# Dividing the queries, folding the sums into the projection, and a column of ones for the softmax denominators

## The chip, the cores and the metric

The kernel runs on one core of a Trainium2 chip. The metric is the device time of one execution in microseconds (us). Before the change the median of three runs is 7744.9 us (7739.69 to 7749.79). The engines are called as in the profile: PE is the matrix engine (PEld its weight loads), DVE the vector engine, ACT the scalar engine, POOL the GpSimd engine, SP the engine that issues most DMAs.

## What is computed

Four images of 256 channels and 64 x 64 pixels (4096 positions) go through four blocks, each added to its input after a group norm: a block with deformable sampling and a feed-forward, linear attention on several scales, a 3 x 3 convolution with binarised weights, and a non-local block with pooled keys. The change touches the second and the fourth:

```python
# layer 1: linear attention, heads of 8 channels
ms = jnp.concatenate([qkv, agg], axis=1)          # qkv, and a 5x5 depthwise aggregate of it
t = ms.reshape(B, -1, 3 * DIM, H * W)
q, k, v = jnp.split(t, 3, axis=2)
q = jax.nn.relu(q)
k = jax.nn.relu(k)
vk = jnp.einsum('bhdn,bhen->bhde', v, k)
out = jnp.einsum('bhde,bhen->bhdn', vk, q)
denom = jnp.einsum('bhe,bhen->bhn', k.sum(-1), q)
out = out / (denom[:, :, None, :] + EPS)
out = out.reshape(B, -1, H, W)
out = conv2d(out, proj_w, 'SAME')                 # 1x1
out = jax.nn.relu(out * proj_bn_scale[:, None, None] + proj_bn_bias[:, None, None])
...
# layer 3: pooled attention, 4096 queries, 1024 keys after a 2x2 max pool
m1 = jnp.einsum('bnc,bcm->bnm', theta1, phi1)
m1 = jax.nn.softmax(m1, axis=2)
m2 = jnp.einsum('bnm,bmc->bnc', m1, gi1)
m4 = _conv1x1(m2.reshape(B, c, H, W), wz_w, wz_b)
return m4 + ox
```

## The kernel before

All numbers are f32. Channels lie on the 128 partitions (256 channels are two groups), positions along the free dimension in blocks of 512 (eight per image).

**The works.** Python generators write the instructions: `sample` (deformable sampling), `feedforward`, `layer1` (linear attention), `layer2` (the convolution), `layer3` (pooled attention). `beside` (L1182) runs a leading generator and advances others beside it in proportion to costs that they yield. In the ordered stages the order on PE, DVE, ACT and POOL is the order of writing; nothing is reordered on an engine later. The end of the program (the last convolution with the end of the third image's work, and the last pooled attention) is left to a scheduler.

**The stages.** Sampling of image 0 stands beside the first convolutions of images 1 to 3; of image 1 beside feed-forward and linear attention of image 0; of images 2 and 3 beside feed-forward and linear attention of the image before and convolution plus pooled attention of the image before that. After sampling come the feed-forward and linear attention of image 3, from the latter's start beside the convolution and pooled attention of image 2, then the convolution and the pooled attention of image 3.

**Sampling** is 288 rounds per image, each of four indirect DMAs that POOL issues (L591) into one of seven buffers g. PE multiplies each g into acc (L598); ACT copies acc to at every second round (L603), which frees a half of acc; PE transposes at (L608). When all seven buffers are in use, POOL waits for the matmuls of L598.

**Linear attention.** `rows` (L790) makes q, k and v per block (matmuls L805) into padded tiles pad; `depthwise` (L169) runs the 5 x 5 aggregate, 25 steps per chunk of 1024 positions on DVE (L178). Other work is put into a list `later`, one entry of which is written out between the DVE steps. `outer` (L842) transposes keys and values (L850, L851) and adds their products over positions into `sums` (L857). `summed` (L869) runs once when the sums of a tile index t are complete, for kind 0 (qkv) and kind 1 (aggregate): it masks the sums to the head blocks (`ln`, L873) and lays the key sums out as weights `ld`. `output` (L879) runs per chunk of 1024 queries: `dens` makes the denominators (matmul L889, on DVE an add and a reciprocal into rd); then for each half h, four `head` entries and two `proj` entries. A head multiplies ln with the queries (num, L898), spreads the reciprocals over the channels of a head (rden, L901), copies num to ot on ACT (L903) and multiplies ot with rden on DVE (L904). `proj` multiplies four ot with the projection weights pw (L910), and ACT (pr, L912) and DVE (L913) finish. There are 32 heads per image, 128 in all.

**Pooled attention.** `first` and `then` make th (queries), ph (keys) and gt (values). Then for each tile of 128 queries (32 per image): scores s against 1024 keys (L1135), their maxima on DVE (L1136, L1137), the exponential on ACT with its sums accumulated (L1142), eight transposes on PE (L1150), two copies on ACT (L1151), eight matmuls with gt (L1155), and on DVE the sum of two partial denominators (L1144), the reciprocal (L1145) and the scaling of the result into m2 (L1156). After four tiles, L1161 multiplies m2 with the output weights.

**PSUM.** The mm pool has three banks, taken in turn by `ps()`: num, rden, s, pt, ps, po and the others share them, and a matmul waits until whoever read the bank three takings before has finished.

## Time and profile before

| | us |
|---|---|
| median of three runs | 7744.9 |
| profiled execution, its own time | 7735.88 |
| its span, first to last instruction | 7734.1 |
| PE busy (share of the span) | 5939.0 (77%) |
| DVE busy | 5191.6 (67%) |
| POOL busy | 5026.2 (65%) |
| ACT busy | 2200.4 (28%) |
| gathers L591: first to last start | 133.2 to 6250.0 |
| num matmuls L898, all forms, records summed | 161 |
| ACT copies L903 | 75.0 |
| DVE multiplies L904 | 87.4 |
| PE waits for the copies at L603 (acc <- ACT) | 711.0 |
| ACT waits for num | 333.4 |

Busy times are those of records. An f32 matmul leaves two records that overlap, so PE's busy time is larger than its work. A share of the whole span is a mean over stages that are bound by different engines; the stages have to be read one by one. "A waits for B" is idle time of A that ended when B's instruction finished.

### The profile page before, as it was taken

The numbers are of one execution on the slowest core, as the hardware profiler recorded it, in microseconds if no ns is written. First come the engines' busy times: TensorE is split into PE (matmuls) and PEld (weight loads), VectorE is DVE, ScalarE is ACT, GpSimd is POOL, SyncE is SP. The second block draws the span as 40 slices with busy tenths as digits, with TensorE's granted clock in tenths as the row PEclk, the third lists the DMA queues.
The fourth block names the chain that finished last, engine by engine and source line by source line (L and its number), as shares of the span: only waits on it lengthen the run. The fifth ranks groups of instructions, "written<-read, shape, count | busy, mean of one in ns | idle before, by whom it ended". The sixth has DMA issues, their size and how long they took to land. (4 is left out here: it accounts for less than half of the span.)

```text
span 7734.1 us, 94959 instructions
## 1 busy us (share of the span) xinstructions
PE 5939.0 (77%) x36000; PEld 3468.1 (45%) x36000; DVE 5191.6 (67%) x6665; ACT 2200.4 (28%) x4879; POOL 5026.2 (65%) x4870
## 2 busy tenths in 40 slices
PE   5666666579766677898777778987777889967899
PEld 2333333334333333446544434465444435744487
DVE  6555553644787887238888892289888933999634
ACT  1111111212222222223233222222333323655415
POOL 2777777777777777777777667777776621966220
PEclk7676776779777778999898899998888999978999
DMA  6564664565544444555544455465444432210121
GB/s 188 152 178 137 172 173 139 160 183 157 162 122 125 125 141 132 165 151 163 149 144 133 122 154 165 136 170 157 142 134 128 123 123 65 75 52 33 63 87 58
DMA packets 744344, 1031.45 MB, mean 133 GB/s; under 512 B 354128, under 2 KB 459984, under 8 KB 742352
## 3 DMA queue, kind: packets, MB, share of 16 engines
q0 software_dynamic: 221184, 604.27, 27.2%
q1 hardware_dynamic: 522704, 421.10, 18.2%
q8 instruction: 285, 4.67, 0.3%
q14 instruction: 171, 1.40, 0.1%
HBM read 856.39 MB, written 168.61 MB: 133 GB/s over the span
## 5 line engine op out<-in xcount | busy, mean ns | idle before, releaser
L591 POOL DMA_INDIRECT g<-tab,sl x4608 | 4492.3, 975 | 1757.4 <-issue 1273.2
L178 DVE SCALAR_TENSOR_TENSOR agg<-pad,vec,agg 128x1024 f32<-128x1024 f32 x2280 | 2934.0, 1287 | 60.6
L598 PE MATMUL acc<-g,wm 128*32 128x128 f32 x18432 | 1266.6, 319 | 1241.6 <-ACT at L603 711.0
L598 PEld LDWEIGHTS acc<-g,wm 128*32 128x32 f32 x18432 | 623.2, 121 | 1927.9 <-ACT at L603 951.2
L1036 PE MATMUL ps<-xd,w 128*128 128x256 f32 x3072 | 712.3, 385 | 7.3 <-DVE x L1016 2.8
L582 DVE TENSOR_TENSOR wm<-con,sl 128x768 f32<-128x768 f32 x384 | 365.8, 953 | 420.3 <-PE acc L598 400.7
L1036 PEld LDWEIGHTS ps<-xd,w 128*128 128x128 f32 x3072 | 577.6, 193 | 107.3 <-issue 29.8
L618 ACT COPY dT<-dp 64x128 f32<-64x128 f32 x1152 | 296.7, 258 | 1044.3 <-PE dp L608 705.6
L730 PE MATMUL ps<-x2f,f 128*128 128x512 f32 x1024 | 479.0, 615 | 4.0 <-ACT f L705 4.0
L740 PE MATMUL ps<-hm,f 128*128 128x512 f32 x1024 | 462.0, 600 | 0.0
L715 DVE SCALAR_TENSOR_TENSOR hm<-ps,vec,lk 128x512 f32<-128x512 f32 x256 | 192.2, 751 | 400.4 <-ACT lk L732 397.3
L805 PE MATMUL ps<-xr,qw 128*128 128x512 f32 x768 | 450.7, 718 | 11.5 <-DVE ot L904 4.1
L987 POOL TENSOR_TENSOR xd<-xp 128x640 f32<-128x640 f32 x64 | 79.5, 1269 | 477.3 <-ACT xp L999 382.9
L603 ACT COPY at<-acc 128x256 f32<-128x256 f32 x576 | 214.4, 372 | 490.0 <-PE acc L598 477.9
L732 ACT ACTIVATE lk<-ps,low 128x512 f32<-128x512 f32 x256 | 175.9, 687 | 594.9 <-PE ps L730 593.6
L631 PE MATMUL po<-dT,ow 128*128 128x288 f32 x1024 | 312.2, 455 | 13.4 <-ACT dT L626 6.5
L608 PE MATMUL dp<-ident,at 128*128 128x128 f32 x1152 | 267.6, 320 | 66.8 <-ACT dT L618 54.7
L194 POOL TENSOR_TENSOR ak<-ak,m 128x1024 f32<-128x1024 f32 x96 | 228.1, 2376 | 131.0 <-ACT m L193 126.7
L1155 PEld LDWEIGHTS ps<-gt,pT 128*128 128x128 f32 x2048 | 278.5, 215 | 60.7 <-issue 34.3
L1155 PE MATMUL ps<-gt,pT 128*128 128x128 f32 x2048 | 291.0, 302 | 7.1 <-ACT pT L1151 7.0
L730 PEld LDWEIGHTS ps<-x2f,f 128*128 128x128 f32 x1024 | 191.3, 194 | 230.1 <-issue 216.9
L194 POOL TENSOR_TENSOR av<-av,m 128x1024 f32<-128x1024 f32 x96 | 226.9, 2363 | 101.1 <-ACT m L193 96.7
(246 smaller groups left out, 7723.0 us busy)
## 6 DMA issues: line engine op xcount, KB each, us to landing
g<-tab,sl POOLq DMA_INDIRECT x4608
x<-x SPq DMA_DIRECT2D x128, 512.0 KB
xr<-x SPq DMA_DIRECT2D x96, 512.0 KB
tab<-xo SPq DMA_DIRECT2D x192, 128.0 KB
x<-in_x SPq DMA_DIRECT2D x32, 512.0 KB
y<-yc SPq DMA_DIRECT2D x32, 512.0 KB
yb<-y SPq DMA_DIRECT2D x64, 256.0 KB
x<-yb SPq DMA_DIRECT2D x64, 256.0 KB
```

Of the source, the lines that this page charges most:

```text
L178: nc.vector.scalar_tensor_tensor(to, s, wt, acc, ALU.mult, ALU.add)
L194: nc.gpsimd.tensor_tensor(acc, acc, m, ALU.add)
L582: nc.vector.tensor_tensor(wm, self.con("own").unsqueeze(1).unsqueeze(1).to_broadcast(sh), blocks[b][:, r:r + WR, G:].unsqueeze(3).to_broad ...
L591: nc.gpsimd.indirect_dma_start(out=g[:, i, :], out_offset=None, in_=table, in_offset=bass.IndirectOffsetOnAxis(ap=sl.bitcast(I32)[:, r, i: ...
L598: nc.tensor.matmul(acc[32 * i:32 * i + 32, :], wm[:, r4, 4 * i + 2 * x:4 * i + 2 * x + 2, :], g[:, i, x * P:(x + 1) * P], start=x == 0, st ...
L618: nc.scalar.copy(dT[b][hs, :, r:r + UR], dp[u][hs, :, :, s, :].rearrange("p v g o -> p g v o"))
L631: nc.tensor.matmul(po[m][:, 0:BR * OB], self.ow[:, k, m * P:(m + 1) * P], dT[b][:, k].rearrange("p r o -> p (r o)"), start=k == 0, stop=k ...
L730: nc.tensor.matmul(ps, f1[:, k, m * P:(m + 1) * P], x2[:, k], start=k == 0, stop=k == KT - 1)
L740: nc.tensor.matmul(ps, f2[:, k, m * P:(m + 1) * P], hm[:, k], start=k == 0, stop=k == 4 * KT - 1)
L805: nc.tensor.matmul(ps, qw[:, k, m * P:(m + 1) * P], x[:, k], start=k == 0, stop=k == KT - 1)
L1036: nc.tensor.matmul(ps[:, e], w[:, k, t, 2 * half + e, m * P:(m + 1) * P], v[:, 2 * half + e, k, t:t + 8], start=i % 6 == 0, stop=i % 6 == 5)
L1155: nc.tensor.matmul(ps[:, 0:P], pT[:, m], gt[:, m], start=m == 0, stop=m == 7)
```

## The change

In linear attention the order of the factors is swapped when the sums are formed, so that they come out as values by keys. `summed` multiplies each masked sum into the 128 rows of the projection weights that belong to it (comb), and copies the product over pw. A head then has no num matmul and no ACT copy: DVE multiplies the queries with the spread reciprocals, and the projection runs on these. `ld` and the denominators stay as they are.

In pooled attention gt gets a 129th column of ones. The result's matmul is 129 columns wide, and its last column is the denominator; the exponential doesn't accumulate any more, DVE has only a reciprocal of that column, and ACT scales the result into m2.

```diff
                 def added(i):
                     for j in range(2):
-                        nc.tensor.matmul(sums[:, t, kind], kts[i][:, 0, j], kts[i][:, 1, j],
+                        nc.tensor.matmul(sums[:, t, kind], kts[i][:, 1, j], kts[i][:, 0, j],
                                          start=first and i + j == 0, stop=last and i + 1 == len(at) and j == 1,
                                          skip_group_check=True)
...
             def summed(t):
 
+                pc = self.ps("comb").rearrange("p (e o) -> p e o", e=2)
                 for kind in range(2):
                     j = 2 * kind + t
                     nc.vector.tensor_tensor(ln[:, j], sums[:, t, kind], self.con("bd"), ALU.mult)
...
+                for kind in range(2):
+                    nc.tensor.matmul(pc[:, kind], ln[:, 2 * kind + t], pw[:, 2 * kind + t], start=True, stop=True)
+                    nc.vector.tensor_copy(pw[:, 2 * kind + t], pc[:, kind])
...
                 def head(h, j):
                     if not j:
                         xv.append(self.block(bp, self.x3_d[n], 2 * c + h, "xq", bufs=1))
-                    pn = self.ps("num")
-                    nc.tensor.matmul(pn, ln[:, j], qh[h][j], start=True, stop=True)
                     hs, i = slice(64 * (j // 2), 64 * (j // 2) + 64), 2 * h + j % 2
                     pb = self.ps("rden")
                     nc.tensor.matmul(pb, self.con("sel")[hs, i * P:(i + 1) * P], rd[0][hs], start=True, stop=True)
                     ot[h, j] = bp.tile([P, 512], F32, name="ot", tag="kt", bufs=4)
-                    nc.scalar.copy(ot[h, j], pn)
-                    nc.vector.tensor_tensor(ot[h, j], ot[h, j], pb, ALU.mult)
+                    nc.vector.tensor_tensor(rw(ot[h, j]), qh[h][j], rw(pb), ALU.mult)
...
-            gt = sp.tile([P, 8, P], F32, name="gt")
+            gt = sp.tile([P, 8, P + 1], F32, name="gt")
+            nc.vector.memset(gt[:, :, P:], 1.0)
...
-                nc.vector.tensor_tensor(gt[:, b], ps[:, P:2 * P], gb, ALU.add)
+                nc.vector.tensor_tensor(gt[:, b, 0:P], ps[:, P:2 * P], gb, ALU.add)
...
                     pe = bp.tile([P, M], F32, name="pe")
-                    den = bp.tile([P, 3], F32, name="den3")
                     for i in range(2):
-                        nc.scalar.activation(pe[:, i * 512:(i + 1) * 512], s[i], AF.Exp, bias=mx[:, 2:3], accum_out=den[:, i:i + 1])
+                        nc.scalar.activation(pe[:, i * 512:(i + 1) * 512], s[i], AF.Exp, bias=mx[:, 2:3])
                     yield 2
-                    nc.vector.tensor_tensor(den[:, 2:3], den[:, 0:1], den[:, 1:2], ALU.add)
-                    nc.vector.reciprocal(den[:, 2:3], den[:, 2:3])
...
                     ps = self.ps()
                     for m in range(8):
-                        nc.tensor.matmul(ps[:, 0:P], pT[:, m], gt[:, m], start=m == 0, stop=m == 7)
-                    nc.vector.tensor_scalar(m2[:, j * P:(j + 1) * P], ps[:, 0:P], den[:, 2:3], None, ALU.mult)
+                        nc.tensor.matmul(ps[:, 0:P + 1], pT[:, m], gt[:, m], start=m == 0, stop=m == 7)
+                    rden = bp.tile([P, 1], F32, name="rden")
+                    nc.vector.reciprocal(rden, ps[:, P:P + 1])
+                    nc.scalar.activation(m2[:, j * P:(j + 1) * P], ps[:, 0:P], AF.Copy, scale=rden)
```

The yields and their costs are unchanged, and so is the order of all other instructions in the ordered stages. In the unordered end the scheduler's order on PE and ACT moves a little around the tiles of pooled attention.

## The prediction

> **What bounds the kernel now.** I read the page's slices first, then who GpSimd (POOL) waits for in stretches, then busy time by stretch, then the groups that the change touches. First the slices (each digit tenths of 193 us):

> ```profile
> PE   5666666579766677898777778987777889967899
> DVE  6555553644787887238888892289888933999634
> POOL 2777777777777777777777667777776621966220
> PEclk7676776779777778999898899998888999978999
> ```

> POOL issues the gathers of sampling. One takes 0.946 us and the next starts about 0.30 us later, so 76 us busy in 100 is its full pace, and slices 2 to 32 are paced by it as long as it keeps that pace. The 6s and single low windows are where it didn't. Who held it (us, times, longest), in 2700-3160, 4200-4700 and 5800-6260 us:

> ```profile
> POOL g L591 <- issue: 102.0, 335, 0.3
> ...
> POOL g L591 <- PE acc L598: 0.3, 1, 0.3
> ...
> POOL g L591 <- issue: 88.0, 289, 0.3
> POOL g L591 <- PE acc L598: 69.3, 32, 7.6
> ...
> POOL g L591 <- issue: 82.5, 271, 0.3
> POOL g L591 <- PE acc L598: 67.3, 30, 6.5
> ```

> The reader is to see that the same attention output costs nothing in the second image's sampling (0.3 us of wait), and that in the third's and fourth's, where the pooled attention runs as well, POOL runs out of gather buffers for 69 and 67 us, because TensorE is late. Busy time of PE, PE loads, DVE, ACT, POOL by stretch:

> ```profile
> 3900.00:4000.00 100.00, 65.55 (x533) 44.14 (x531) 91.97 (x113) 32.77 (x82) 76.24 (x79) 0.89 0.46 132
> 4400.00:4500.00 100.00, 81.41 (x502) 43.59 (x501) 85.75 (x110) 33.12 (x78) 59.63 (x62) 0.91 0.44 127
> 6000.00:6100.00 100.00, 87.56 (x526) 46.48 (x525) 85.71 (x103) 31.95 (x75) 65.25 (x68) 0.92 0.41 117
> 6950.00:7000.00 50.00, 35.52 (x146) 23.36 (x147) 48.92 (x54) 32.20 (x50) 34.88 (x15) 0.90 0.13 43
> 7050.00:7100.00 50.00, 47.08 (x142) 23.82 (x143) 45.62 (x53) 23.93 (x36) 22.83 (x10) 0.94 0.13 42
> 7650.00:7700.00 50.00, 50.00 (x294) 39.90 (x293) 24.72 (x65) 28.53 (x66) 0.00 (x0) 1.00 0.19 64
> ```

> At 4400 and 6000 no engine is full: PE, DVE and ACT wait for each other in a fixed order. At 6950 (sampling over) DVE is full; at 7050, with attention output, PE and DVE share the bound; at 7650 PE is full. The groups:

> ```profile
> L898 PE MATMUL num<-pad,ln 128*128 128x512 f32 x128 | 79.5, 704 | 1.5 <-ACT pT L1151 1.1 <-DVE ot L904 0.4
> L903 ACT COPY ot<-num 128x512 f32<-128x512 f32 x128 | 75.0, 586 | 333.6 <-PE num L898 333.4
> L904 DVE TENSOR_TENSOR ot<-ot,rden 128x512 f32<-128x512 f32 x128 | 87.4, 683 | 94.8 <-PE rden L901 90.7 <-ACT yb L642 4.1
> L1142 ACT ACTIVATION_READ_ACCUMULATOR pe<-s,mx 128x1 f32 x256 | 50.4, 197 | 0.0
> L1156 DVE TENSOR_SCALAR m<-ps,den 128x128 f32<-128x128 f32 x128 | 44.6, 349 | 110.6 <-PE ps L1155 110.0
> ```

> ACT stands 333 us waiting for num: not work, but while it waits, the copies of acc behind it (L603) are late, and PE waited 711 us for those.

> [...] two 512-column f32 matmuls of L1161 (four records of about 0.6 us each) take 1.72 us from start to next start, so one costs 0.86 us at full clock, and I price with that, not with the records. [...] sixteen records of L1155 take 1.78 us, 0.111 each for 128 columns, so a 129th column is an estimated 0.9 ns per record. [...]

> **The change part by part.**

> *Heads (32 per image).* Gone: one 512-column matmul (0.86 us, about 0.95 at the clock of 0.9 there), one ACT copy (0.586) and one of two PSUM banks taken from a rotation of three. The DVE multiply stays; its source is now q (partly strided rows) and no longer waits for ACT. I keep 0.68, bounds 0.62 to 0.75.

> *Summed (2 per image).* New: two comb matmuls of 256 columns (630 records of L1036 in 135.99 us: 0.43 per matmul), two DVE copies from PSUM (L1019's 0.42), and DVE waits some 0.7 for the first. About 1.5 each, 3 us per image where DVE is full. If PE is behind, a wait like the 5 us seen elsewhere comes in: bound 10. PE in turn waits at comb for DVE, with the acc matmuls behind it; seven gather buffers cover that.

> *Pooled tiles (32 per image).* DVE loses an add (0.154), a reciprocal (0.163) and the scaling (0.350), and gains a reciprocal from PSUM, not shown before: 0.16 like L1145's, bounds 0.13 to 0.25. Net -0.50. ACT loses two accumulator reads (0.2 each, about 0.08 each of pitch, as the next exp overlaps them) and gains a 128-element scaled copy[...]. PE gains 16 x 0.9 = 14 ns; bounds 0 and, should an odd row length cost, double, 1.8 us. The new ACT copy waits for DVE's reciprocal; behind it on ACT stand the next exp and L603, for which PE waits. A memset is once per image.

> Now by stage, since a microsecond counts only where it isn't under POOL.

> First two samplings: POOL at full pace, or no touched code. 0.

> Third sampling. num has 43 records in 4300-4600, two per matmul, so 21 heads: 21 x 0.95 = 20 us of PE, 21 x 0.586 = 12 of ACT, and 12 tiles (96 transposes) x 0.50 = 6 of DVE. POOL is short of its pace by 12.3+16.7+11.6 busy us there, 53 us of time. These overlap in one ring, so I count the largest, 20. Before it, 3800-4300, POOL lacks 22 busy us, 29 of time, DVE the fullest; 20 tiles x 0.50 = 10, of which I take 8, one window being at full pace. Sum 28.

> Fourth sampling, the same reading: 24 heads in 5900-6200 give 23, I take 22; the tiles before 8. Sum 30.

> After sampling. DVE full in 6900-7250: 21 tiles x 0.50 = 10.5. In 7000-7345 DVE waits 18.8 us for rden and 31.3 for ACT's pr, which waits for PE; about 35 of the 50 lie before 7250, and PE has 22 of the 32 heads (19 us) less there: I take 15. In 7250-7350 PE has 46.9 and 42 of 50; 10 heads x 0.86 = 8.6. Less 3 for summed. Sum 31. What is late next: the depthwise chains on DVE, then PE.

> The last pooled attention, 196 us, is full on PE: +32 x 0.014 = 0.5, and 0.3 for reciprocal plus ACT copy in the tail. Its DVE and ACT savings are hidden by PE; without that cover they would be worth 16 us.

> Sum: -28 -30 -31 +1 = -88. The profiled execution took 7735.9 (span 7734.1), so 7648; the median of the runs, 7744.9, stands 9 above it, so **7657 us**. With each share taken low (heads 8 per stage, tiles 4, after sampling 12) it is -36; taken high (heads 35, tiles 15, after 45), -145: 7709 and 7600.

> **Rivals.**

> *DVE keeps the bound.* The 85 to 92 in 100 of DVE say that it sets most rounds and PE's saving falls in gaps. Then 12+11 tiles and the tiles before count half (14), after sampling 10.5+8.6, less 3 per image in stages that count (9), and half of the wait relief (8): about -32, 7713. Against: where DVE alone is busy (3900) POOL is at full pace; it falls only where heads come in.

> *The ring opens.* If the copy that stalled ACT was the hinge, most of the 53+29 us and the like of the fourth sampling come back, some 100, with 50 after: -150, 7595. For: the 711 us of PE waits on L603. Against: DVE at 86 leaves little.

> *The new ACT copy takes the place of the old.* In order on ACT, it waits until DVE reaches the reciprocal, often behind three taps of 1.29 us (3.9). If 96 tiles lose 1.3 us each to late L603 copies, that is +125-88 = +37, 7782. It decides from 0.92 us per tile. For: DVE is the lagging engine. Against: ACT already waits for DVE's maxima in 95 of 128 tiles (339 us), and the reciprocal stands before the next maxima in DVE's order; ACT is busy a third of the time.

> *The waits only change name.* Gathers stay as late for another reason: 7745.

> **How the numbers follow.** Forecast 0.50, DVE keeps the bound 0.20, ring opens 0.15, ACT copy 0.10, no effect 0.05. Within 0.2% (15 us) a measurement can't be told from no change. Faster is the sum of the first three, 0.85; same 0.05; slower 0.10. The range 7600 to 7735 leaves out the ACT copy and no effect (0.15) and the far part of the open ring (0.05).

> **What would show it.** Right: POOL's waits for acc fall from 69 and 67 to about 45 each; ACT has no 333 us before ot; DVE's busy falls by about 64 us less 7; the last gather starts some 55 us before 6250; the last 196 us stay within 2. Wrong: a long ACT wait for DVE's reciprocal with PE waiting on L603 more than 711; L1155 records over 0.12 us; DVE still at 98 in 100 with the same end; PEclk lower where PE got work taken away.

## The result, and the profile after

| | before | after |
|---|---|---|
| median, us (ten runs each) | 7746.37 | 7758.41 |
| lowest to highest, us | 7739.69 to 7757.17 | 7748.26 to 7775.53 |
| ratio after/before, 95% interval | | 1.0017 [1.0007, 1.0027] |
| profiled execution, us | 7735.88 | 7748.26 |
| last gather starts at, us | 6250.0 | 6283.4 |
| mean granted clock of PE | 0.851 | 0.839 |

A gain of 88 us was forecast; the change lost 12, less than 0.2%. Both profiled executions took some 10 us less than the median of their kernel. The work that was to go has gone. These are the page's busy times of after (busy us, share of the span, instructions) and, of its slices, the row of PE's granted clock (tenths, one digit per 194 us):

```profile
PE 5899.6 (76%) x35776; PEld 3468.2 (45%) x35776; DVE 5126.8 (66%) x6429; ACT 2148.7 (28%) x4623; POOL 5035.0 (65%) x4870
...
PEclk7676776779777677999888888999888889988999
```

DVE's busy time fell by 65 us (57 forecast) and ACT's by 52. PE has 224 matmul records fewer (256 for num gone, 32 for comb and the like come), but its busy time fell by only 39 us, though the num records alone summed to 161. The PEclk row (before's stands in the prediction) hints at the reason: of slices 17 to 34, eleven read 9 before and seven after. The windows below show it sharper.

Who waits for whom in after, over the span (total us, times, longest us):

```profile
PE acc L598 <- ACT at L603: 711.4, 370, 26.2
ACT m L1157 <- DVE rden L1156: 361.0, 108, 15.3
POOL g L591 <- PE acc L598: 297.7, 182, 11.2
```

ACT's 333 us before ot are gone. In their place stand 361 us before m: ACT waits for DVE's late reciprocal, up to 15.3 us at a time, with the copies of acc behind it. PE's wait for those copies has stayed where it was (711.0 before). POOL's wait for PE has risen (269.8 before), not fallen; in the two stretches where the forecast had 69 and 67 us and expected 45, it is 85 and 81.

Where the time went, stage by stage. The marks are the starts of gathers, counted from 0, so that the stretches hold the same sampling in every kernel: "pooled" is where pooled attention stands beside sampling, "crowded" where linear attention's heads stand there too. Each of the first two rows is one profiled execution, so differences below some 5 us mean little by themselves.

| us | third: pooled (2880-3136) | third: crowded (3136-3456) | fourth: pooled (4032-4300) | fourth: crowded (4300-4607) | last gather to last pooled attention | last stage |
|---|---|---|---|---|---|---|
| before | 331.3 | 467.4 | 344.4 | 448.3 | 1315.2 | 168.9 |
| after | 337.8 | 482.6 | 349.5 | 462.8 | 1287.1 | 175.9 |
| difference | +6.5 | +15.2 | +5.1 | +14.5 | -28.1 | +7.0 |

Before gather 2880 and between the two groups of stretches, after gains 8 us. So these four stretches, which were to give 58 us, took 41 more, and the last gather starts 33 us later; the stretch after them gave what was forecast; the last stage took 7 more. The two crowded stretches by windows, before (length, then busy time of PE, PE loads, DVE, ACT and POOL with counts, granted clock, DMA share, GB/s):

```profile
4221.70:4689.10 467.40, 364.42 (x2396) 197.33 (x2396) 382.82 (x452) 141.22 (x343) 309.47 (x320) 0.88 0.46 137
5801.70:6250.00 448.30, 346.03 (x2278) 184.72 (x2276) 369.03 (x437) 134.49 (x326) 296.61 (x307) 0.89 0.43 128
```

and after:

```profile
4221.80:4704.40 482.60, 356.11 (x2340) 198.22 (x2340) 377.78 (x421) 128.36 (x296) 313.19 (x321) 0.83 0.44 133
5820.60:6283.40 462.80, 341.49 (x2242) 188.42 (x2241) 366.05 (x409) 122.44 (x283) 299.97 (x307) 0.83 0.42 124
```

Less work on PE, DVE and ACT, a longer stretch, and a clock of 0.83 where it was 0.88 and 0.89.

### The profile page after: what moved, and what is told of

The parts are those of the page before. It is cut to its first block, busy times and chain, and to the rows that moved or that the text cites. A ratio compares the mean times of both kernels' runs of the same rounds, so it can differ in the third digit from the quotient of the medians.

```text
span 7746.5 us, 94023 instructions
## 1 busy us (share of the span) xinstructions
PE 5899.6 (76%) x35776; PEld 3468.2 (45%) x35776; DVE 5126.8 (66%) x6429; ACT 2148.7 (28%) x4623; POOL 5035.0 (65%) x4870
## 5 line engine op out<-in xcount | busy, mean ns | idle before, releaser
L591 POOL DMA_INDIRECT g<-tab,sl x4608 | 4502.1, 977 | 1781.0 <-issue 1267.5
L598 PE MATMUL acc<-g,wm 128*32 128x128 f32 x18432 | 1288.4, 322 | 1248.4 <-ACT at L603 711.4
L598 PEld LDWEIGHTS acc<-g,wm 128*32 128x32 f32 x18432 | 631.2, 122 | 1955.1 <-ACT at L603 941.0
L603 ACT COPY at<-acc 128x256 f32<-128x256 f32 x576 | 214.1, 372 | 488.6 <-PE acc L598 474.3
L732 ACT ACTIVATE lk<-ps,low 128x512 f32<-128x512 f32 x256 | 175.9, 687 | 595.5 <-PE ps L730 595.5
L1154 PE MATMUL ps<-gt,pT 128*128 128x129 f32 x2048 | 303.6, 310 | 7.3 <-ACT pT L1150 6.9
L1137 PE MATMUL s<-ph,th 128*128 128x512 f32 x512 | 274.2, 649 | 22.8 <-DVE r L1164 6.3
```

The lines of the kernel that those rows point to most:

```text
L591: nc.gpsimd.indirect_dma_start(out=g[:, i, :], out_offset=None, in_=table, in_offset=bass.IndirectOffsetOnAxis(ap=sl.bitcast(I32)[:, r, i: ...
L598: nc.tensor.matmul(acc[32 * i:32 * i + 32, :], wm[:, r4, 4 * i + 2 * x:4 * i + 2 * x + 2, :], g[:, i, x * P:(x + 1) * P], start=x == 0, st ...
L1137: nc.tensor.matmul(s[i], tv[:, 4 * b + j], ph[:, i * 512:(i + 1) * 512], start=True, stop=True)
L1154: nc.tensor.matmul(ps[:, 0:P + 1], pT[:, m], gt[:, m], start=m == 0, stop=m == 7)
```

## The experiments

Three things had to be told apart: what the linear half does by itself, what the pooled half does, and what made the last stage longer. Two theories stood for the first: that PE's removed work is given back by a lower granted clock, or that PE was never the bound there and only waits changed name.

The runs landed at two levels. In one group of sessions the kernel before took about 7750 us, in another about 8800. The ratios are always against runs of before in the same session. The expectations below call the two levels a first and a second kind of chip; that the chip makes the level isn't shown. The kernels that decide were run at the first level, which is that of the result; the second level is told first and kept apart.

### At the level of 8800 us

**Only the linear half** (after, with before's pooled attention):

```diff
-            gt = sp.tile([P, 8, P + 1], F32, name="gt")
+            gt = sp.tile([P, 8, P], F32, name="gt")
...
-                        nc.scalar.activation(pe[:, i * 512:(i + 1) * 512], s[i], AF.Exp, bias=mx[:, 2:3])
+                        nc.scalar.activation(pe[:, i * 512:(i + 1) * 512], s[i], AF.Exp, bias=mx[:, 2:3], accum_out=den[:, i:i + 1])
...
-                    nc.scalar.activation(m2[:, j * P:(j + 1) * P], ps[:, 0:P], AF.Copy, scale=rden)
+                    nc.vector.tensor_scalar(m2[:, j * P:(j + 1) * P], ps[:, 0:P], den[:, 2:3], None, ALU.mult)
```

> The linear-attention half alone (divided queries, sums folded into the projection); pooled attention as before. ACT-copy theory (the loss in the crowded samplings comes from ACT's new scaling waiting for DVE's reciprocal, which holds up the copies of acc): the loss is gone, last gather at 6200 to 6225 us, time about 7680. Clock theory (with the num matmuls gone PE's granted clock falls and eats the saving): last gather still 6260 to 6285, clock 0.835 to 0.842, time 7740 to 7760. DVE theory (DVE sets these stretches, so linear attention gains nothing there): last gather 6245 to 6255, time about 7725.

**Only the pooled half** (after, with before's `outer`, `summed` and `head`):

> The pooled half alone (column of ones, scaling on ACT); linear attention as before, with its num matmuls and ACT copies. ACT-copy theory: the loss is here and larger than in the whole change, last gather 6280 to 6310, time 7755 to 7790. Clock theory: DVE's half microsecond per tile counts and the clock stays at 0.851, last gather 6220 to 6245, time about 7715. DVE theory: the same direction, last gather about 6230, time about 7720. The last pooled attention takes about 7 us longer than before in all of them, 176 instead of 169 us, since that stage holds no other part of the change.

**The whole change, with the result scaled on DVE instead of ACT:**

```diff
-                    nc.scalar.activation(m2[:, j * P:(j + 1) * P], ps[:, 0:P], AF.Copy, scale=rden)
+                    nc.vector.tensor_scalar(m2[:, j * P:(j + 1) * P], ps[:, 0:P], rden, None, ALU.mult)
```

> The whole change, but the result of a tile is scaled on DVE as before (reciprocal and scaling on DVE, column of ones kept). ACT-copy theory: last gather 6205 to 6230, time about 7675. Clock theory: as the whole change in the samplings, last gather 6265 to 6285, clock 0.84, time 7740 to 7760. DVE theory: 0.35 us more DVE per tile, last gather about 6255, time about 7735. The last pooled attention back to about 169 us if its 7 us came from the ACT scaling; still 176 if they came from the 129th column or from the exponential without sums.

**The whole change with the num matmul put back in its own bank.** Its product is not read, so this is PE work and a bank only:

```diff
+                    pn = self.ps("num")
+                    nc.tensor.matmul(pn, ln[:, j], qh[h][j], start=True, stop=True)
```

> The whole change, with the num matmuls put back as dead work (their result isn't read; the ACT copies stay away), so PE has its old load and bank takings. Clock theory: clock back to about 0.85, and the samplings as fast as in the whole change or faster, last gather 6255 to 6285. ACT-copy theory: PE gets 20 us per image more in a ring that is late already, last gather 6300 or later, clock between, time 7790 or more. DVE theory: last gather unchanged at 6283 within 5, time about 7775 from the 20 us in the stretch after sampling.

Measured against 8807.45 us: linear half 0.9952 [0.9936, 0.9969], pooled half 1.0011 [0.9998, 1.0023], scaled on DVE 0.997 [0.9958, 0.9983], num back 1.0015 [1.0005, 1.0025]. These didn't fit the result: the parts were faster or the same, and the whole had been slower. So after itself was run again, with three more.

**After again, and before again:**

> The changed kernel itself, once more, beside the others of this group. All theories: 1.0017 of the kernel before within 0.0015. It gives the stretch times on the same chip as the next three.

> The kernel before, once more, for its trace on the same chip: time within 0.3% of its other runs here. ACT-copy theory: between gather 2880 and the last, the changed kernel is 30 to 45 us later than this one, the early reciprocal 30 to 60 us earlier. Clock theory: both are later.

**The linear half with before's sums and reciprocal, but the scaling on ACT.** The reciprocal is then made early, before the transposes, so ACT needn't wait for DVE there:

```diff
-                    nc.vector.tensor_scalar(m2[:, j * P:(j + 1) * P], ps[:, 0:P], den[:, 2:3], None, ALU.mult)
+                    nc.scalar.activation(m2[:, j * P:(j + 1) * P], ps[:, 0:P], AF.Copy, scale=den[:, 2:3])
```

> The linear half, with the old pooled attention except that ACT scales the result, with the reciprocal that DVE made early from the summed exponentials. ACT's scaling waits for PE alone here, no longer for DVE at the end of its queue. If it is the late reciprocal that holds ACT up: no loss against the linear half alone, 0.995 of the kernel before within 0.002. If any scaling on ACT costs it (ACT stands behind PE's eight matmuls while copies of acc wait): 1.000 to 1.003, like the whole change. If the loss had nothing to do with ACT: 0.995 too, but then the scaling on DVE in the whole change should have brought nothing, and it brought about 0.4%.

**The whole change, scaled on DVE, with the exponential still accumulating its sums in the last stage.** Nothing reads those sums (`wide` is true in the last stage alone):

```diff
+                    den = bp.tile([P, 3], F32, name="den3") if wide else None
                     for i in range(2):
-                        nc.scalar.activation(pe[:, i * 512:(i + 1) * 512], s[i], AF.Exp, bias=mx[:, 2:3])
+                        more = {"accum_out": den[:, i:i + 1]} if wide else {}
+                        nc.scalar.activation(pe[:, i * 512:(i + 1) * 512], s[i], AF.Exp, bias=mx[:, 2:3], **more)
```

> The whole change with the result scaled on DVE, and in the last pooled attention (only there) the exponential accumulates its sums as before, though nobody reads them. The order of PE in the last stage is then the regular one of before: scores, transposes, scores, result. Order theory for the last 7 us: that stage takes 169 us instead of 176, and the time is 0.996 of the kernel before, the scaling on DVE having had 0.997. If the 129th column cost it, 176 and 0.997.

Against 8794.03 us: after again 0.9982 [0.9972, 0.9993], early reciprocal on ACT 0.997 [0.9957, 0.9982], sums kept 0.996 [0.9943, 0.9977]; before again 8792.53 us in a single execution, within the spread of its others.

So at this level the same change is a gain of 0.18%, and the linear half one of 0.48%. The num matmul put back in its own bank makes the whole change 0.33% slower here (two sessions, each against its own before), with the mean clock going from 0.796 to 0.805: against what the clock theory expected, it was not free. Compare the dead matmul without a bank at the other level, below; whether the bank or the level makes the difference no run separates. The waits of before again show that this level is another regime: instead of the owner of a buffer, the releaser named is often "remote" (one that the view has no name for), which the waits at the first level don't have among their large rows (total us, times, longest us):

```profile
ACT dT L618 <- remote: 629.5, 70, 21.2
...
POOL g L591 <- remote: 549.5, 268, 4.2
```

There the compute engines stand still together, 124 times for over 1 us and 279 us in all, mostly in the first half of the execution; at the first level before has 4 such gaps, 22 us. These runs can't explain the result. What makes the level is open.

### The two halves, at the level of the result

The linear half again, and the pooled half with its scaling on DVE (edits as above):

> The linear half alone again, on another chip: the time of the kernel before showed two levels on the chips so far (7746 and about 8800 us), and the loss of the whole change was seen at 7746 only. If this chip is of the first kind: ACT-copy theory 0.990 to 0.994 of the kernel before, with the crowded stretches (gathers 3136 to 3456 and 4300 to 4607) shorter than 467 and 448 us; clock theory 0.998 to 1.002, crowded stretches 480 and 460 as in the whole change. On a chip of the second kind: 0.995 within 0.002, as before.

> The pooled half alone, scaled on DVE: column of ones, but linear attention as before. ACT-copy theory: better than the pooled half with the scaling on ACT (1.0011 on a chip of the second kind) by 0.001 to 0.003, so 0.998 to 1.000; the last stage still 176 us. If the scaling on ACT costs nothing where the num copies are on ACT too: 1.001 or above, since DVE has 0.35 us per tile more.

Linear half 1.0002 [0.9994, 1.0011], pooled half on DVE 0.9983 [0.9976, 0.999], both against 7750.37 us. The linear half, to which the forecast gave about 60 of the 88 us, is worth nothing. Its crowded stretches in the third and the fourth sampling:

```profile
4235.20:4705.20 470.00, 356.01 (x2339) 200.68 (x2340) 382.42 (x454) 123.79 (x308) 310.44 (x320) 0.82 0.45 136
5820.90:6274.00 453.10, 341.76 (x2238) 191.71 (x2237) 370.51 (x440) 119.31 (x298) 297.17 (x308) 0.82 0.42 126
```

The clock is 0.82, where before has 0.88 and 0.89. The clock theory had expected longer stretches, 480 and 460 us. The groups by line show it in the matmuls that both kernels have. First before, in the third sampling's crowded stretch (counts, busy us, mean ns of one record, idle before it):

```profile
L598 PE MATMUL acc<-g,wm 128*32 128x128 f32 x1360 | 61.9, 306 | 65.0 <-ACT at L603 65.0
...
L901 PE MATMUL rden<-rd,con 64*128 64x512 f32 x64 | 38.3, 680 | 6.9 <-DVE rd L892 3.2 <-ACT ot L903 2.0 <-ACT pe L1142 1.6
```

then the linear half alone:

```profile
L598 PE MATMUL acc<-g,wm 128*32 128x128 f32 x1360 | 68.4, 323 | 62.0 <-ACT at L603 59.6 <-DMA g<-tab,sl 2.3
...
L903 PE MATMUL rden<-rd,con 64*128 64x512 f32 x64 | 43.9, 772 | 8.8 <-DVE rd L896 4.7 <-DVE ot L905 3.5 <-DVE den L1145 0.6
```

The same 1360 gather matmuls have records of 323 ns instead of 306, the 64 for rden 772 instead of 680. These two groups take 6.5 and 5.6 us more; of the lines left out here, those of the projection's and the pooled result's matmuls went from 55.7 to 63.8 and from 40.6 to 46.0. That is 25.6 us in four groups. The num records that went summed to 39 us in this stretch, and PE's busy time fell by 8.4.

A record could also be longer because num no longer runs just before it. The clock intervals in the traces, whose mean the views print, rule that out: they are at full or at half speed and nothing between. In the third's crowded stretch the clock is at half for 113 us in before and for 169 in the linear half. The rden records that run wholly at full speed take 639 ns in before and 641 in the linear half, those wholly at half 1130 and 1136; of the 64, 4 run at half in before and 16 in the linear half. The starts agree: from the first record of a matmul to its second are 533 ns at full speed and 1015 at half. So the mean is longer because the clock is low during more of them.

### Is it the clock?

If the lower clock comes from PE having less to do, then work that nobody needs should bring it back, and should cost nothing until the clock has recovered. If PE was simply not the bound, the work costs nothing either, but whatever it does to the clock, and a second piece should be as free as the first. So the linear half was given one, then two, matmuls per head of num's shape, written into the bank that rden then overwrites; their products are not read, and there is no copy and no further bank (the second kernel has range(2)):

```diff
                     pb = self.ps("rden")
+                    for _ in range(1):
+                        nc.tensor.matmul(pb, ln[:, j], qh[h][j], start=True, stop=True)
                     nc.tensor.matmul(pb, self.con("sel")[hs, i * P:(i + 1) * P], rd[0][hs], start=True, stop=True)
```

> The linear half with one dead matmul per head (sums times queries, overwritten by the next matmul in the same bank): PE's old work, without the old bank and ACT copy. Clock theory: the granted clock is back to 0.85 (0.88 in the crowded stretches), and the time is that of the linear half within 0.001. Ring theory: the same time too, clock also up. Neither would be right if the time rises by 0.003 or more with the clock up: then PE's work counts fully and the clock's fall had cost nothing.

> The linear half with two dead matmuls per head, so more matrix work than before the change. Clock theory: the clock is full already with one, so the second costs its work where PE counts: 20 us in each of the two crowded stretches and 15 to 25 after sampling, time 1.005 to 1.008 of the kernel before. Ring theory (PE's work isn't what sets these stretches): within 0.002 of the run with one.

One: 1.0004 [0.9994, 1.0014], so 128 matmuls of about 0.9 us, 115 us of PE work, cost nothing that the intervals show. Two: 1.0037 [1.0023, 1.0052], so the second 128 cost 24 us, between what the two theories expected. The crowded stretches of the third and the fourth, with one:

```profile
4225.40:4692.20 466.80, 369.89 (x2407) 200.94 (x2408) 381.76 (x454) 123.94 (x308) 311.39 (x320) 0.88 0.46 137
5807.70:6257.70 450.00, 354.52 (x2304) 190.22 (x2303) 369.81 (x440) 119.44 (x298) 298.93 (x308) 0.88 0.43 127
```

with two:

```profile
4228.80:4698.40 469.60, 382.68 (x2447) 206.45 (x2448) 381.98 (x453) 123.67 (x308) 310.99 (x320) 0.90 0.46 137
5820.70:6273.00 452.30, 366.34 (x2338) 195.59 (x2340) 369.98 (x439) 118.47 (x296) 297.97 (x307) 0.90 0.43 126
```

The clock is 0.82 without, 0.88 with one, 0.90 with two, in both samplings. The groups of the third follow, with one:

```profile
L598 PE MATMUL acc<-g,wm 128*32 128x128 f32 x1360 | 64.2, 313 | 55.4 <-ACT at L603 55.2 <-DMA g<-tab,sl 0.2
...
L905 PE MATMUL rden<-rd,con 64*128 64x512 f32 x64 | 38.1, 677 | 3.1 <-DVE rd L896 3.1
```

and with two:

```profile
L598 PE MATMUL acc<-g,wm 128*32 128x128 f32 x1344 | 61.2, 306 | 55.1 <-ACT at L603 55.1
...
L905 PE MATMUL rden<-rd,con 64*128 64x512 f32 x63 | 36.1, 652 | 2.3 <-DVE rd L896 2.3
```

rden's records take 772, 677, 652 ns as PE gets more to do: the dead work makes the live work faster. By the clock intervals 16, 4 and 1 of them run at half speed, and the stretch is at half for 169, 113 and 96 us. That the clock follows PE's work, and the live matmuls the clock, is thereby shown for these stretches. How steeply the clock follows no run settles: PE's busy share of the third's crowded stretch is 76, 79 and 81 in 100 in the three, and part of that is the matmuls' own length.

That the time follows the clock isn't shown. The crowded stretches of the three kernels, at 0.82, 0.88 and 0.90, take 470.0, 466.8 and 469.6 us, and 453.1, 450.0 and 452.3 in the fourth: within the 5 us that mean little. The whole change scaled on DVE has the same 0.83 there as after, and the length of before:

```profile
4229.90:4697.20 467.30, 351.45 (x2339) 198.79 (x2340) 382.53 (x437) 121.74 (x277) 308.74 (x321) 0.83 0.46 137
```

By the forecast's reckoning the second matmul should have cost as much as the first should have gained, 42 us in the crowded stretches alone; it cost 24 in all, and in the crowded stretches only 2.8 and 2.3 in the profiled executions (7.4 lie between the last gather and the last pooled attention, the rest is spread). So PE's work counts there for little even at a clock of 0.88, with DVE busy for 382 of 467 us. Two things thus stand against the forecast's 20 us per sampling: the clock falls and takes PE's saving back, and PE's time isn't what sets these stretches, as the rival "DVE keeps the bound" has it. Which would have been enough alone, these runs don't separate.

### Who scales the result, and when

Three places for the scaling with the linear half in: on DVE with the whole change, on ACT with the early reciprocal, and on ACT with the late one, which is after itself. And ACT with the early reciprocal alone, in the kernel before:

> The whole change with the result scaled on DVE, again. On a chip of the first kind: ACT-copy theory 0.992 to 0.996, crowded stretches shorter than 467 and 448 us; clock theory 1.000 to 1.002. On a chip of the second kind: 0.997 within 0.0015.

> The linear half with ACT scaling by the early reciprocal, again. On a chip of the first kind: if only the late reciprocal holds ACT up, as the linear half alone within 0.001; if any scaling on ACT does, 0.003 or more above it. On a chip of the second kind: 0.997 within 0.0015.

> The kernel before with one edit: ACT scales the pooled result, by the reciprocal that DVE makes early. If DVE's 0.35 us per tile counts and ACT has room: 0.997 to 0.999 of the kernel before, with the gain after sampling (DVE full there), 32 tiles x 0.35 = 11 us, and up to 10 in the samplings. If ACT waiting behind PE's result holds up the copies of acc also with its num copies present: 1.000 or above.

| | ratio | third crowded | fourth crowded |
|---|---|---|---|
| linear half, scaled on DVE, sums (as before) | 1.0002 [0.9994, 1.0011] | 470.0 | 453.1 |
| whole change, scaled on DVE | 0.9996 [0.9987, 1.0004] | 467.3 | 451.0 |
| linear half, ACT, early reciprocal | 0.9979 [0.9969, 0.9989] | 471.4 | 453.7 |
| whole change = ACT, late reciprocal | 1.0017 [1.0007, 1.0027] | 482.6 | 462.8 |
| before with ACT, early reciprocal | 1.0017 [1.001, 1.0025] | 476.2 | 456.8 |

Scaled on DVE, the two halves alone (1.0002 and 0.9983) would give 0.9985 together, and the whole change is at 0.9996; the intervals allow both.

Each stretch is one execution, from 10 us below its kernel's median (after) to 10 above it (early reciprocal). With the late reciprocal, the move of the scaling from DVE to ACT (second row to fourth, one edit) costs 15 and 12 us in the crowded stretches and 0.2% of the whole; with the early one (first row to third, one edit) it costs about 1 and gains 0.23%. Early and late on ACT differ by 11 and 9 us there. They differ by 0.38% of the whole, but these two kernels also differ in the sums and in the last stage, where 7 us lie. The waits of the early kernel (total us, times, longest us):

```profile
POOL g L591 <- PE acc L598: 276.3, 165, 10.9
ACT m L1157 <- PE ps L1156: 244.9, 80, 12.5
```

ACT waits for PE's product instead of for DVE behind it, 245 us instead of 361, and POOL's wait for PE is 276 where after has 298. This kernel is faster than both before and after: 7735.98 us. The last row of the table shows that the move to ACT isn't good by itself: beside the old num copies it costs 0.17%, without them it gains 0.23% on the linear half alone. The 11 us that its expectation promised after sampling didn't come either: that stretch is 7 us longer than in before. The likeliest reading is that the linear half makes room on ACT, and only another move turns that into time; no run takes the copies away and leaves all else.

### The last stage

The last pooled attention took 175.9 us instead of 168.9. At the level of the result it was longer in every kernel without the exponential's sums, wherever it scaled (whole change on DVE 177.0, pooled half on DVE 175.6), and shorter in those that keep them (linear half 168.9, early reciprocal on ACT 168.9, the same in the kernel before 171.3). One more kernel keeps the sums there, unread, together with the 129th column (the edit of the last kernel of the first group, on the pooled half alone):

> The pooled half alone, scaled on DVE, with the exponential's sums kept (unread) in the last stage only: before the change minus one small add per tile on DVE and minus the accumulator reads on ACT. The last stage is back at 169 us, so 7 us below the same kernel without these sums: 0.997 to 0.998 of the kernel before on a chip of the first kind, 0.998 to 1.000 on one of the second. If the last stage stays at 176, the order of the scheduler wasn't the reason.

0.9986 [0.9977, 0.9994], 7735.3 us against 7746.63, last stage 169.8. So the column with its reciprocal costs 0.9 us (0.5 worked out), and the other 6 come from the absence of the sums: this kernel and the pooled half on DVE differ in nothing else. In the whole the 6 us don't show: the two ratios, 0.9986 and 0.9983, lie within each other's intervals, where 0.0008 less was expected. PE's timeline in before, in the middle of the stage (start, length, instruction):

```profile
7653.27 1.13 PE L1135 MATMUL s<-ph,th 128*128 128x512 f32 x2
7654.23 1.04 PE L1150 MATMUL pt<-ident,pe 128*128 128x128 f32 x8
7655.10 1.13 PE L1135 MATMUL s<-ph,th 128*128 128x512 f32 x2
7656.07 1.95 PE L1155 MATMUL ps<-gt,pT 128*128 128x128 f32 x16
```

and in after:

```profile
7662.51 1.13 PE L1137 MATMUL s<-ph,th 128*128 128x512 f32 x2
7663.47 0.60 PE L1149 MATMUL pt<-ident,pe 128*128 128x128 f32 x4
7663.91 2.00 PE L1154 MATMUL ps<-gt,pT 128*128 128x129 f32 x16
7665.74 1.99 PE L1137 MATMUL s<-ph,th 128*128 128x512 f32 x4
7668.58 1.23 PE L1137 MATMUL s<-ph,th 128*128 128x512 f32 x2 [0.85 <-DVE mx L1138]
```

Before: scores (2 records), transposes (8), scores (2), result (16), in turn. After: the transposes split into fours, scores pile up in a run of six, and PE then waits for DVE's maxima. PE's waits for them over the stage, first before, then after (total us, times, longest us):

```profile
PE s L1135 <- DVE mx L1136: 0.8, 1, 0.8
...
PE s L1137 <- DVE mx L1138: 4.2, 5, 0.9
```

The stage is unordered; the program's scheduler put it so once the exponentials had no sums to deliver.

## Why the prediction was wrong

*What failed first: removed PE work counted as time.* "21 x 0.95 = 20 us of PE", and 22 in the fourth sampling, took the removed matmuls at the clock that the stage had, and took all of PE's saving as saving of the stage. The linear half, in which these matmuls are gone, measured 1.0002, with crowded stretches no shorter than before's (2.6 and 4.8 us longer in one execution each). The clock went from 0.88 and 0.89 to 0.82, and 25.6 of 39 us of records came back in other matmuls of one stretch. And with the clock at 0.88 to 0.90 a matmul more per head costs these stretches 2 to 3 us, not 20. For the first point the forecast had named a sign ("PEclk lower where PE got work taken away") but gave it no chance and no rival; for the second it had "DVE keeps the bound" at 0.20, which still expected a gain of 32 us. In the third and fourth samplings it wrote -28 and -30; measured were +22 and +20.

*What failed second: the wait of the new ACT copy, in size.* The forecast gave "The new ACT copy takes the place of the old" a tenth. It was there in all parts: ACT waits 361 us for DVE's reciprocal, the copies at L603 are late behind it. Its price is 20 us in the two crowded stretches together against the early scaling on ACT and 27 against scaling on DVE, far below the 88 at which the rival was to decide. With that gain gone, it decides the sign: after is at 1.0017, the whole change with DVE scaling at 0.9996. The argument used against it, that "the reciprocal stands before the next maxima in DVE's order", left out what stands before the reciprocal.

*The ACT copies.* With one dead matmul per head back, the linear half differs from before chiefly by the missing copies and by what DVE waits for, and measures 1.0004. The 333 us of ACT's wait for num were worth nothing; ACT then waits longer for DVE's maxima. Over the span, first before, then the linear half:

```profile
ACT pe L1142 <- DVE mx L1137: 339.1, 95, 15.6
...
ACT pe L1143 <- DVE mx L1138: 445.5, 102, 18.5
```

The rival "waits only change name" was right for this part, at a chance of 0.05.

*After sampling:* -31 forecast, -28.1 measured; that the sum came so near is in part luck. Its terms aren't confirmed. DVE's busy time there fell by 35 us (867.0 to 832.0), where 32 tiles at 0.50 make 16; the forecast took the add at its median, 0.154, but the records of these adds have a mean of 0.298 over the program and go up to 2.3 us. And busy time isn't time: the linear half alone gives -1.9 there in its profiled execution, the pooled half on DVE -3.3, the whole change on DVE -8.7. Why all of it together with ACT's scaling gives 28 stays open.

*The last stage:* "+1" for columns and tail, +7.0 measured. The column was about right (0.9 with 0.5 forecast). The step left out is that a scheduler's order may change with an output that nobody needs.

*Right:* DVE's busy time (57 forecast, 65 measured), the reciprocal from PSUM (0.165 us measured, 0.16 forecast), ACT's 333 us gone, summed's wait (one of 5.3 us at comb in the third sampling, where "the 5 us seen elsewhere" was named), and records of the result's matmul, 276 ns in the last stage with 128 and with 129 columns. The new ACT copy takes 0.367 us; the forecast had only the author's estimate for it.

## What to carry to other kernels

Don't price removed matmuls at the clock that the profile shows when PE isn't full and the clock isn't 1.0: read the PEclk column of that stage first, and allow that all of it comes back (here 25.6 of 39 us of records did in one stretch, and the stretch was no shorter: 470.0 us against 467.4). A kernel with as much dead work put back, and one with twice as much, show how far the clock follows (0.82, 0.88, 0.90 here) and whether PE's work sets the stage at all (470.0, 466.8, 469.6 us). Before an operation is moved to another engine whose order is fixed, look at which engine makes its last operand and how late that stands there: the same move of a scaling to ACT, in kernels without the num copies, was worth -0.2% with an early scale and +0.2% with a late one. Where a scheduler sets the order, an output that nothing reads can hold a good order (a last stage of 169.8 us with it, 175.6 without), so compare the order of the engine that is full.
